# A Macaron block: down products summed up in three PSUM banks, one stretch of seven, other orders of blocks and loads

## The chip, the cores and the metric

The kernel runs on one core of a Trainium2 chip, in one launch. The metric is the device time in microseconds. It is given as the median of several runs; the profiled execution is one more run, with the hardware profiler on.

## The reference

All is in fp32. There are 8 sequences of 512 tokens with 512 features, and every sequence passes three layers one after another:

```python
x = x + 0.5 * ffn(layernorm(x), w_gate, w_up, w_down)
x = x + attention(layernorm(x), W_q, W_k, W_v, W_o)
x = x + 0.5 * ffn(layernorm(x), w_gate, w_up, w_down)      # same weights as above

def ffn(x, w_gate, w_up, w_down):                          # 512 -> 2048 -> 512
    h = silu(x @ w_gate) * (x @ w_up)
    g = h.reshape(..., 512, 4)
    h = keep the two of each four with the largest magnitude, 0 for the others
    return h @ w_down

def attention(x, ...):                                     # 16 heads of 32, 4 heads of K and V
    Q, K, V = x @ W_q, x @ W_k, x @ W_v                    # rotary embedding on Q and K
    return (softmax(Q @ K.T / sqrt(32)) @ V) @ W_o         # 16 query heads on 4 kv heads
```

## The kernel before, in words

**Blocks.** A feed-forward of one sequence is a block, so there are 16: `(b, 0)` is the first of sequence b, `(b, 1)` the second. The list `blocks` (L90) sets their order. Attention of a sequence and the layer norms of later blocks run beside the blocks as side stages: Python generators, one step at a time. The loop at L1047 takes the main groups of a block from `ffn` and advances a counter `n` by the group's size (1 stands for a full group of 8 fp32 matmuls with 256 columns, 0.5 for half of it). After each group, a side stage goes one step on when `n` has passed its due time. A block has `WIDTH = 42` units. `sides` (L1003) holds the first and last `n` of each stage: the layer norm of a block runs from 15 to 2 units before the block, and attention b in a window that L1007 to L1017 compute; a start more than 17 units into a block is moved to the next block's start.

**A planner writes every engine's order down.** `takes`, `waits`, `soon`, `later` and `fill` keep an estimate of when TensorE, VectorE (DVE) and ScalarE are free. DVE work that TensorE waits for goes into the queue `urgent`, other work into `put_off` and `for_later`. `fill` emits DVE work where the estimate says that it ends in time, and thinning steps last. `ensure` emits everything up to an entry at once. Each engine then runs in the order written down, and semaphores keep the data safe.

**Gate and up.** A block has four chunks c of 512 hidden features (`NCH = 4`), each with two woven pairs (`woven`, L613). A pair does two row groups as seven half-size products in place of eight (Strassen's scheme in Winograd's form). Their weights are quarters of w_gate and w_up or sums of quarters; the sums are made in the first block on DVE (`combine_gu`, L688, L693), stored in DRAM and later read from there. A pair holds a PSUM bank x through all of it, a bank v from its second to its fourth product, and a bank z near its end. There are three such banks for everything but attention's scores and outputs (`Bank`, L225, hands out the one that is free first).

**Thinning.** `keep_two_of_four` (L393) zeroes two of each four values of h, in two halves of 256 tokens: comparisons of magnitudes, then four `scalar_tensor_tensor` (L440) on DVE. It starts at the end of a chunk (`begin`, L757), which also emits every step that is left of the thinning before. At the end of a half, POOL (GpSimd) makes sums of quarters of h (L446 to L451).

**Down.** Two chunks together, an even and an odd one, make a pair g of chunks. Its product with w_down is again done as seven half-size products (`PRODUCTS`, L476, `products`, L532), each 8 matmuls into one bank, 3.45 us. 31 of the 32 pairs go this way; the last goes as plain products (`down`, L577). The right sides are quarters of w_down or sums of them (`SUMS`, L485), made once by POOL (`combine_down`, L492, L505) and kept in DRAM. `down_weights` (L510) loads them into three buffers: the load for product i+3 is issued after product i. Each product is added to one or two quarters of the tokens on DVE (L565), 12 additions for a pair. A quarter of h or of w_down is named by its row and column ("21" is the second row's first). The products of a pair are `owed`: `some(n)` yields the next n. Two of them stand inside the second woven pair of the following even chunk (after its fourth and fifth product), five after it.

**Attention** (L772). Side steps: loads (`wqkv`, `cs`), layer norm with transposes into `xT`, five projections and V, then for each of four groups of heads four steps of scores, maxima (`nm`, DVE), exponentials (ScalarE), weighted sums and a sum of exponentials (`total`, DVE), and at last four products with W_o. `xT` is one of two buffers that the blocks use too; the list `in_xT` lets no third one in. `p_slots` has two larger buffers (`cs`, `total`, `p`, and `raw` at the start); `wqkv` and `wo` share one.

All DMAs are issued by SP (SyncE), in the order written.

Of the kernel before, what the change touches and what calls it, by code (L numbers as in the profile page):

```python
# [26 lines left out]
def macaron_block(  # L27
# [62 lines left out]
    blocks = [(0, 0), (1, 0)]  # L90
    for b in range(2, B):
        blocks += [(b, 0), (b - 2, 1)]
    blocks += [(B - 2, 1), (B - 1, 1)]
# [184 lines left out]
    def layernorm_t(got, tag, src=None, xb=None):  # L278
# [34 lines left out]
        def turn(t):  # L313
            if t == 0:
                assert len(in_xT) < 2
                in_xT.append(got)
                got["xT"] = xtp.tile([P, ND, S], FP, tag="xT", name="xT")
            xT = got["xT"]
            tr = transposed([xn[t][:, c * P : (c + 1) * P] for c in range(ND)])
            nc.scalar.copy(xT[:, :, t * P : (t + 1) * P], tr.tile)  # L320
            tr.free(end=takes("act", 0.6, pe_heard()))
# [11 lines left out]
        if xb is None:  # L333
            there = at["pe"] + 10.0
            yield lambda: there
            found = [soon(0.9, partial(moments, t)) for t in (0, 1)]
            yield now
            found += [soon(0.9, partial(moments, t)) for t in (2, 3)]
            yield partial(when, found[:2])
            ensure(found[:2])  # L340
            scales((0, 1))
            yield partial(when, found)
            ensure(found)
            scales((2, 3))
            yield by_scalar
            for t in range(NT):
                normalise(t)
                end = at["act"]
                yield by_scalar if t < NT - 1 else lambda: max(end, by_scalar()) if len(in_xT) < 2 else None
# [43 lines left out]
    def keep_two_of_four(h, made, sums=None, halves=(0, 1)):  # L393
# [14 lines left out]
        for half in halves:  # L408
# [32 lines left out]
            if sums is not None:  # L441


                (h11, h21), (h12, h22) = ([h[:, i::2, :HALF], h[:, i::2, HALF:]] for i in range(2))
                if half == 0:
                    nc.gpsimd.tensor_tensor(sums[:, 2], h11, h12, ALU.add)  # L446
                else:
                    nc.gpsimd.tensor_tensor(sums[:, 1], h21, h22, ALU.add)
                    nc.gpsimd.tensor_tensor(sums[:, 0], h11, h22, ALU.add)
                    nc.gpsimd.tensor_tensor(h12, h12, h22, ALU.subtract)  # L450
                    nc.gpsimd.tensor_tensor(h21, h21, h11, ALU.subtract)  # L451
# [11 lines left out]
    def begin(steps):  # L463
# [20 lines left out]
    )  # L484
    SUMS = ("11+22", "12-22", "21-11", "11+12", "21+22")  # L485
# [6 lines left out]
    def combine_down(g):  # L492

        for c in range(2 * g, 2 * g + 2):
            raw = p_slots.tile([P, 4, D], FP, "raw")
            nc.sync.dma_start(out=raw, in_=w_down[c])
            there = at["pe"] + 12.0
            yield lambda: there
            yield now
            quarter = {f"{i + 1}{j + 1}": raw[:, i::2, j * HD2 : (j + 1) * HD2] for i in range(2) for j in range(2)}  # L500
            sums = wa_slots.tile([P, 6, 2, HD2], FP, "sums")

            for i, name in enumerate(SUMS):
                op = ALU.add if name[2] == "+" else ALU.subtract
                nc.gpsimd.tensor_tensor(sums[:, i], quarter[name[:2]], quarter[name[3:]], op)  # L505
                nc.sync.dma_start(out=combined[g, name][:, c % 2 * 2 : c % 2 * 2 + 2, :], in_=sums[:, i])
            yield now
        done_down.add(g)

    def down_weights(g, name):  # L510
        w = wdp.tile([P, 4, HD2], FP, tag="wd", name="wd")
        if (g, name) in combined:
            nc.sync.dma_start(out=w, in_=combined[g, name])
        else:
            i = int(name[0]) - 1
            for q in range(2):
                nc.sync.dma_start(
                    out=w[:, 2 * q : 2 * q + 2, :], in_=w_down[2 * g + q][:, i::2, i * HD2 : (i + 1) * HD2]
                )
        return w  # L520

    def ffn(b, final, last):
# [9 lines left out]
        def products(hs, g):  # L532

            operands = []
# [6 lines left out]
            def product(i):  # L541
                name, _, quarters = PRODUCTS[i]
                y = Bank([P, 2, HD2], "y")
                for t in range(2):
                    for n in range(4):
                        h, e = hs[n // 2]
                        if name in ("11+22", "21+22", "11+12"):
                            part = e[:, ("11+22", "21+22", "11+12").index(name), n % 2, :]
                        else:
                            row, col = int(name[0]) - 1, int(name[1]) - 1  # L550
                            part = h[:, 2 * (n % 2) + col, row * HALF : (row + 1) * HALF]
# [4 lines left out]
                            start=(n == 0),  # L556
                            stop=(n == 3),
                        )
# [4 lines left out]
                def add(half, side, sign, ends):  # L563
                    to = xb[:, 2 * half : 2 * half + 2, side * HD2 : (side + 1) * HD2]
                    nc.vector.scalar_tensor_tensor(to, y.tile, 0.5 * sign, to, ALU.mult, ALU.add)  # L565
                    if ends and g == NCH // 2 - 1 and i >= 5:
                        store(xb, (0, 1) if i == 5 else (2, 3))

                fill()
                y.free([soon(0.62, partial(add, *to, to == quarters[-1])) for to in quarters])  # L570
                written[b, final] = y.slot[1]
# [3 lines left out]
            return [(1 if i < 2 else 2, partial(product, i)) for i in range(len(PRODUCTS))]  # L575
# [112 lines left out]
        def combine_gu(i):  # L688
# [3 lines left out]
            def one(j, a, b, op):  # L692
                nc.vector.tensor_tensor(w[j], a, b, op)  # L693
                nc.sync.dma_start(out=gu_sums[i][:, j - S1], in_=w[j])

            gu_made[i] = [
                later(0.62, partial(one, j, w[a], w[b], op), at["pe"], for_later)
# [10 lines left out]
        for c in range(NCH):  # L708
# [27 lines left out]
            else:  # L736
                for pair in range(2):
# [7 lines left out]
                    for k, g in enumerate(groups):  # L745
                        yield g
                        if k == 2 and opens and i + 1 < 2 * NCH:
                            combine_gu(i + 1)

                        if pair == 1 and c % 2 == 0 and k in (3, 4):  # L750
                            yield from some(1)
# [4 lines left out]
                    if pair == 1:  # L756
                        begin(keep_two_of_four(h, list(last_one), e))  # L757
                        yield from some(5, False)
# [13 lines left out]
    def attention(b):  # L772
        ensure(written[b, 0])
        wa = wa_slots.tile([P, ND, D + 2 * KV], FP, "wqkv")
        for src, col in ((w_k, D), (w_q, 0), (w_v, D + KV)):
            nc.sync.dma_start(
                out=wa[:, :, col : col + src.shape[1]], in_=src.rearrange("(c p) n -> p c n", p=P)
            )
        cs = p_slots.tile([P, 4, S], FP, "cs")
        nc.sync.dma_start(out=cs[:, :2, :], in_=rope.rearrange("a p s -> p a s"))  # L780
        got = {}
        yield from layernorm_t(got, "xa", tokens[b][1])
# [5 lines left out]
        def projected(dst, col, scale):  # L788
# [16 lines left out]
            return [p_slots.used(w_slots.used(made))]  # L805
# [20 lines left out]
        in_xT.remove(got)  # L826
# [3 lines left out]
        nc.sync.dma_start(out=wo[:, :, :D], in_=w_o.rearrange("(c p) n -> p c n", p=P))  # L830
# [90 lines left out]
        for t in range(NT):  # L921
            found = scores(0, t, nm)
            yield partial(when, found)
# [79 lines left out]
    sides = [(11, 18, 6, partial(combine_down, 0), None, None), (22, 32, 6, partial(combine_down, 1), None, None)]  # L1003
# [3 lines left out]
    before = 0  # L1007
    for b in range(B):
# [6 lines left out]
        assert last - first > ATTENTION * 0.8  # L1015
        sides.append((first, last, ATTENTION, partial(attention, b), ("attention", b - 1) if b else None, ("attention", b)))
        before = last  # L1017
# [101 lines left out]
```

## Time and profile before

| what | us |
|---|---|
| median of three runs (3221.35 to 3228.51) | 3227.9 |
| the profiled execution: its time | 3222.35 |
| the profiled execution: span from first to last instruction | 3220.5 |
| TensorE (PE) matmul busy | 3180.1 |
| VectorE (DVE) busy | 2281.7 |
| ScalarE (ACT) busy | 1182.0 |
| GpSimd (POOL) busy | 608.1 |

The profile shows one execution. "Busy" is the time in which at least one instruction of an engine runs. In a row of a group the text before the bar names the line, the engine, the operation, what it writes and reads, its shape and the number of instructions; after it stand the busy time in all and the mean of one in ns; then the idle time of the engine just before these instructions, and what ended most of it. An fp32 matmul appears as two records. In a row of waits stand the waiting engine and tile, what it waited for, the total in us, how often, and the longest. A row of windows gives the stretch and its length, busy time (and instructions) of PE, weight load, DVE, ACT and POOL, the granted clock of TensorE, the DMA engines' busy share and GB/s. The granted clock is 0.999 over the span. A row of the timeline has the start, the length, the engine, the line and the instructions merged in it.

### The profile page before, as it was taken

How to read it: one execution, taken by the hardware profiler on the slowest of the kernel's cores; microseconds unless marked ns; L12 is line 12 of the kernel's file. 1: busy time of each engine (PE TensorE's matmuls, PEld its weight loads, DVE VectorE, ACT ScalarE, POOL GpSimd, SP SyncE). 2: the span in 40 equal slices, each digit the busy share in tenths (PEclk: the TensorE clock that was granted, in tenths of full speed). 3: DMA queues.
4: the chain of work that ended last, by engine and by line, in shares of the span. 5: the costliest groups of instructions: out<-in, count | busy, mean ns of one | idle time of the engine just before them, and what ended most of it. 6: DMA issues, size and time to landing. Idle time of an engine off the chain costs nothing.

```text
span 3220.5 us, 43674 instructions
## 1 busy us (share of the span) xinstructions
PE 3180.1 (99%) x15880; PEld 2320.9 (72%) x15880; DVE 2281.7 (71%) x4869; ACT 1182.0 (37%) x1669; POOL 608.1 (19%) x888
## 2 busy tenths in 40 slices
PE   8999999999999999999999999999999999999999
PEld 6886668766776677767776668666776668666886
DVE  6867875678577775887578766678577775787554
ACT  2222552145324441354314532145324542255211
POOL 2422011211221112111121112111120122201120
PEclk9999999999999999999999999999999999999999
DMA  7762345433533434434543345333533446234451
GB/s 241 245 215 95 113 145 171 138 116 111 194 111 122 157 121 160 138 125 150 166 140 122 119 155 197 120 108 113 202 102 121 156 124 214 95 112 147 152 172 46
DMA packets 249285, 463.21 MB, mean 144 GB/s; under 512 B 24432, under 2 KB 64368, under 8 KB 248304
## 3 DMA queue, kind: packets, MB, share of 16 engines
q1 hardware_dynamic: 249072, 460.42, 43.3%
q8 instruction: 127, 2.08, 0.3%
q14 instruction: 86, 0.70, 0.1%
HBM read 421.53 MB, written 38.80 MB: 143 GB/s over the span
## 4 chain that ended last, share of the span: by engine, by line
PE 94%; DVE 3%; DMA 1%; ACT 1%; issue 0%; SPq 0%; DVEq 0%; ACTq 0%
PE x L624 26%; PE y L552 23%; PE v L624 13%; PE z L624 6%; PE proj L792 4%; PE sc L838 4%; PE st L871 4%; PE ops L887 4%; PE y L972 3%; PE tr L262 2%; PE gu L599 1%; PE den L903 1%; PE vps L817 1%; PE y L582 1%; PE st L876 1%; DMA xn<-x 1%
## 5 line engine op out<-in xcount | busy, mean ns | idle before, releaser
L624 PE MATMUL x<-ts,w 128*128 128x256 f32 x3000 | 720.2, 383 | 6.2 <-DVE corner L638 5.9
L624 PEld LDWEIGHTS x<-ts,w 128*128 128x128 f32 x3000 | 561.0, 190 | 151.4 <-issue 48.1
L552 PE MATMUL y<-wd,h 128*128 128x256 f32 x1984 | 455.2, 383 | 9.0 <-DVE h L440 6.4
L552 PEld LDWEIGHTS y<-wd,h 128*128 128x128 f32 x1984 | 372.8, 190 | 97.2 <-issue 28.8
L446 POOL TENSOR_TENSOR e<-h 128x512 f32<-128x512 f32 x62 | 96.6, 1559 | 1495.7 <-DVE h L440 1364.5
L164 DVE TENSOR_REDUCE nm<-sc 128x1 f32<-128x512 f32 x512 | 320.8, 683 | 63.5 <-PE sc L838 62.0
L565 DVE SCALAR_TENSOR_TENSOR x<-y,x 128x512 f32<-128x512 f32 x372 | 242.2, 686 | 135.6 <-PE y L552 133.8
L552 PE MATMUL y<-wd,e 128*128 128x256 f32 x1488 | 335.3, 380 | 1.0 <-PE den L903 1.0
L552 PEld LDWEIGHTS y<-wd,e 128*128 128x128 f32 x1488 | 281.3, 190 | 53.5 <-issue 11.0
L164 DVE TENSOR_TENSOR total<-total,p 128x512 f32<-128x512 f32 x384 | 266.2, 734 | 58.2 <-ACT p L879 58.2
L879 ACT ACTIVATE p<-st 128x2048 f32<-128x2048 f32 x96 | 179.6, 1870 | 283.2 <-PE st L876 191.3
L254 ACT ACT_TABLE_LOAD x206 | 264.3, 1283 | 4.4 <-PEq L1108 0.7
L673 ACT ACTIVATE h<-x 128x256 f32<-128x256 f32 x125 | 47.5, 380 | 592.8 <-PE x L624 573.1
L242 ACT COPY row<-x 128x512 f32<-128x512 f32 x210 | 122.9, 585 | 383.2 <-PE x L624 382.3
L624 PE MATMUL v<-ts,w 128*128 128x256 f32 x1000 | 238.8, 382 | 3.5 <-ACT xT L320 2.9
L624 PE MATMUL x<-xT,w 128*128 128x256 f32 x1000 | 239.8, 383 | 0.0
L624 PE MATMUL z<-xT,w 128*128 128x256 f32 x1000 | 239.4, 382 | 0.0
L624 PE MATMUL v<-xT,w 128*128 128x256 f32 x1000 | 239.0, 382 | 0.4 <-ACT corner L242 0.4
L624 PEld LDWEIGHTS x<-xT,w 128*128 128x128 f32 x1000 | 186.4, 190 | 50.8 <-issue 24.0
L624 PEld LDWEIGHTS v<-ts,w 128*128 128x128 f32 x1000 | 187.6, 190 | 46.9 <-issue 15.1
L624 PEld LDWEIGHTS z<-xT,w 128*128 128x128 f32 x1000 | 186.4, 190 | 48.2 <-issue 20.9
L624 PEld LDWEIGHTS v<-xT,w 128*128 128x128 f32 x1000 | 187.3, 190 | 45.5 <-issue 11.8
(109 smaller groups left out, 4114.0 us busy)
## 6 DMA issues: line engine op xcount, KB each, us to landing
w<-gu SPq DMA_DIRECT2D x472, 256.0 KB, 3.3
w<-in_w_gu SPq DMA_DIRECT2D x394, 256.0 KB, 3.3
wd<-wd SPq DMA_DIRECT2D x155, 512.0 KB, 3.8
wd<-in_w_down SPq DMA_DIRECT2D x124, 256.0 KB, 4.9
x<-x SPq DMA_DIRECT2D x64, 256.0 KB, 2.6
xn<-x SPq DMA_DIRECT2D x64, 256.0 KB, 6.9
x<-in_x SPq DMA_DIRECT2D x32, 256.0 KB, 3.4
gu<-w SPq DMA_DIRECT2D x32, 256.0 KB, 2.6
```

The source lines that it names most:

```text
L164: self.does()
L242: nc.scalar.copy(dst, src)
L254: nc.scalar.activation(dummy[:, 1:2], dummy[:, 0:1], f)
L552: nc.tensor.matmul(out=y.tile[:, t, :], lhsT=part[:, t * P : (t + 1) * P], rhs=operands[i][:, n, :], start=(n == 0), stop=(n == 3),)
L565: nc.vector.scalar_tensor_tensor(to, y.tile, 0.5 * sign, to, ALU.mult, ALU.add)
L624: nc.tensor.matmul(out=bank.tile[:, m, :], lhsT=lhs[:, m, k, :], rhs=rhs[:, k, :], start=(first and m == 0 and k == 0), stop=(k == 1), ski ...
L792: nc.tensor.matmul(out=ps.tile, lhsT=wa[:, k, col : col + P], rhs=xT[:, k, :], start=(k == 0), stop=(k == ND - 1))
L838: nc.tensor.matmul(out=sc[:, kv, :], lhsT=qT[rows, c, t * P : (t + 1) * P], rhs=kT[rows, :], start=True, stop=True)
L871: nc.tensor.matmul(out=st[:, kv, :], lhsT=kT[rows, t * P : (t + 1) * P], rhs=qT[rows, c, :], start=True, stop=False)
L879: nc.scalar.activation(p, st, AF.Exp)
L887: nc.tensor.matmul(out=ops[rows, :], lhsT=v[:, t, rows], rhs=p[:, kv, :], start=(t == 0), stop=(t == NT - 1))
L972: nc.tensor.matmul(out=y.tile, lhsT=qT[:, k, t * P : (t + 1) * P], rhs=wo[:, k, :D], start=(k == 0), stop=(k == ND - 1))
```

## The change

The products of a pair of chunks follow another form of the scheme: seven products collect in three banks x, v and z, a bank is written on after it has been added to a quarter of the tokens, and each product is added once: 7 additions for 12. The sums of h are four for five, all after the second half, and the sums of w_down four for five; of w_down itself three quarters are used for two. All seven products stand in one stretch after the woven pair (`some(7)`).

Further: the order of the blocks; attention windows of equal width from one end to the other; attention's `xT` in `p_slots` in place of the blocks' buffers; attention's loads in smaller pieces, one per step; the raw chunks of w_down in four loads each; the sums of gate and up quarters due 3 us later in the planner.

```diff
-    blocks = [(0, 0), (1, 0)]
-    for b in range(2, B):
-        blocks += [(b, 0), (b - 2, 1)]
-    blocks += [(B - 2, 1), (B - 1, 1)]
+    first_of = {0: 0, 1: 1, 2: 2, 3: 3, 5: 4, 8: 5, 9: 6, 11: 7}
+    second_of = {4: 0, 6: 1, 7: 2, 10: 3, 12: 4, 13: 5, 14: 6, 15: 7}
+    blocks = [(first_of[i], 0) if i in first_of else (second_of[i], 1) for i in range(2 * B)]
...
             if t == 0:
-                assert len(in_xT) < 2
-                in_xT.append(got)
-                got["xT"] = xtp.tile([P, ND, S], FP, tag="xT", name="xT")
+                if tag == "xf":
+                    assert len(in_xT) < 2
+                    in_xT.append(got)
+                    got["xT"] = xtp.tile([P, ND, S], FP, tag="xT", name="xT")
+                else:
+                    got["xT"] = p_slots.tile([P, ND, S], FP, "xT")
...
-                (h11, h21), (h12, h22) = ([h[:, i::2, :HALF], h[:, i::2, HALF:]] for i in range(2))
-                if half == 0:
-                    nc.gpsimd.tensor_tensor(sums[:, 2], h11, h12, ALU.add)
-                else:
-                    nc.gpsimd.tensor_tensor(sums[:, 1], h21, h22, ALU.add)
-                    nc.gpsimd.tensor_tensor(sums[:, 0], h11, h22, ALU.add)
-                    nc.gpsimd.tensor_tensor(h12, h12, h22, ALU.subtract)
-                    nc.gpsimd.tensor_tensor(h21, h21, h11, ALU.subtract)
+                (h11, h21), (_, h22) = ([h[:, i::2, :HALF], h[:, i::2, HALF:]] for i in range(2))
+                if half == 1:
+                    nc.gpsimd.tensor_tensor(sums[:, 0], h21, h22, ALU.add)
+                    nc.gpsimd.tensor_tensor(sums[:, 1], sums[:, 0], h11, ALU.subtract)
+                    nc.gpsimd.tensor_tensor(sums[:, 2], h[:, 1::2, :HALF], sums[:, 1], ALU.subtract)
+                    nc.gpsimd.tensor_tensor(h21, h11, h21, ALU.subtract)
...
     PRODUCTS = (
-        ("11", "12-22", ((0, 1, 1), (1, 1, 1))),
-        ("11+12", "22", ((0, 0, -1), (0, 1, 1))),
-        ("22", "21-11", ((0, 0, 1), (1, 0, 1))),
-        ("21+22", "11", ((1, 0, 1), (1, 1, -1))),
-        ("11+22", "11+22", ((0, 0, 1), (1, 1, 1))),
-        ("12-22", "21+22", ((0, 0, 1),)),
-        ("21-11", "11+12", ((1, 1, 1),)),
+        ("11", "11", "x", (0, 0)),
+        (0, "12-11", "v", (1, 1)),
+        (1, "22-T1", "x", (0, 1)),
+        (2, "22", "v", (0, 1)),
+        ("21", "22-12", "x", (1, 1)),
+        ("12", "21", "z", (0, 0)),
+        ("22", "21-T2", "x", (1, 0)),
     )
-    SUMS = ("11+22", "12-22", "21-11", "11+12", "21+22")
+    SUMS = ("12-11", "22-T1", "22-12", "21-T2")
...
-            nc.sync.dma_start(out=raw, in_=w_down[c])
-            there = at["pe"] + 12.0
-            yield lambda: there
-            yield now
+            for r in range(4):
+                nc.sync.dma_start(out=raw[:, r], in_=w_down[c][:, r])
+                there = at["pe"] + 5.0
+                yield now if r < 3 else lambda: there
...
-                y = Bank([P, 2, HD2], "y")
+                first, last = name not in used, name not in [p[2] for p in PRODUCTS[i + 1 :]]
+                if first:
+                    used[name] = Bank([P, 2, HD2], name)
+                else:
+                    waits(ensure(taken[name]))
+                y = used[name]
...
-                            start=(n == 0),
+                            start=(first and t == 0 and n == 0),
...
-                y.free([soon(0.62, partial(add, *to, to == quarters[-1])) for to in quarters])
-                written[b, final] = y.slot[1]
+                taken[name] = [soon(0.62, add)]
+                if last:
+                    y.free(taken[name])
+                written[b, final] = taken[name]
...
-            return [(1 if i < 2 else 2, partial(product, i)) for i in range(len(PRODUCTS))]
+            return [(2, partial(product, i)) for i in range(len(PRODUCTS))]
...
+            there = at["pe"] + 3.0
             gu_made[i] = [
-                later(0.62, partial(one, j, w[a], w[b], op), at["pe"], for_later)
+                later(0.62, partial(one, j, w[a], w[b], op), there, for_later)
...
-                        if pair == 1 and c % 2 == 0 and k in (3, 4):
-                            yield from some(1)
...
-                        yield from some(5, False)
+                        yield from some(7, False)
...
-        for src, col in ((w_k, D), (w_q, 0), (w_v, D + KV)):
-            nc.sync.dma_start(
-                out=wa[:, :, col : col + src.shape[1]], in_=src.rearrange("(c p) n -> p c n", p=P)
-            )
-        nc.sync.dma_start(out=cs[:, :2, :], in_=rope.rearrange("a p s -> p a s"))
+        for src, col in ((w_k, D), (w_v, D + KV)):
+            loads.append((wa[:, :, col : col + KV], src.rearrange("(c p) n -> p c n", p=P)))
+        for i in range(2):
+            loads.append((cs[:, i], rope[i]))
+        for k in range(ND):
+            loads.append((wa[:, k, :D], w_q[k * P : (k + 1) * P, :]))
...
-        yield from layernorm_t(got, "xa", tokens[b][1])
+        for ready in layernorm_t(got, "xa", tokens[b][1]):
+            if loads:
+                dst, src = loads.popleft()
+                nc.sync.dma_start(out=dst, in_=src)
+            yield ready
...
-        nc.sync.dma_start(out=wo[:, :, :D], in_=w_o.rearrange("(c p) n -> p c n", p=P))
...
             found = scores(0, t, nm)
+            nc.sync.dma_start(out=wo[:, t, :D], in_=w_o[t * P : (t + 1) * P, :])
...
-    sides = [(11, 18, 6, partial(combine_down, 0), None, None), (22, 32, 6, partial(combine_down, 1), None, None)]
+    sides = [(10, 19, 10, partial(combine_down, 0), None, None), (22, 34, 10, partial(combine_down, 1), None, None)]
...
-        left = place(B - 1, 1) - 13 - before
-        first = max(before, place(b, 0) + WIDTH + 16)
-        if first % WIDTH > 17:
-            first += WIDTH - first % WIDTH
-        last = min(place(b, 1) - 13, max(before + left / (B - b), first + 1.4 * WIDTH))
+    bounds = [WIDTH + 16 + b * (place(B - 1, 1) - 13 - WIDTH - 16) / B for b in range(B + 1)]
```

More of the change, by code (lines that the diff above doesn't have):

```diff
@@ L89, in macaron_block @@
     gu_sums = [dram.tile([P, 4, 2, ND // 2, P], FP, name=f"gu_{i}") for i in range(2 * NCH)]
-    blocks = [(0, 0), (1, 0)]
-    for b in range(2, B):
-        blocks += [(b, 0), (b - 2, 1)]
-    blocks += [(B - 2, 1), (B - 1, 1)]
+    first_of = {0: 0, 1: 1, 2: 2, 3: 3, 5: 4, 8: 5, 9: 6, 11: 7}
+    second_of = {4: 0, 6: 1, 7: 2, 10: 3, 12: 4, 13: 5, 14: 6, 15: 7}
+    assert B == 8
+    blocks = [(first_of[i], 0) if i in first_of else (second_of[i], 1) for i in range(2 * B)]
     coming = deque()
@@ L348, in layernorm_t @@
                 end = at["act"]
-                yield by_scalar if t < NT - 1 else lambda: max(end, by_scalar()) if len(in_xT) < 2 else None
+                yield by_scalar if t < NT - 1 else (
+                    lambda: max(end, by_scalar()) if tag == "xa" or len(in_xT) < 2 else None
+                )
             for t in range(NT):
@@ L503, in combine_down @@
             for i, name in enumerate(SUMS):
-                op = ALU.add if name[2] == "+" else ALU.subtract
-                nc.gpsimd.tensor_tensor(sums[:, i], quarter[name[:2]], quarter[name[3:]], op)
+                of = quarter[name[3:]] if name[3:] in quarter else sums[:, int(name[4:]) - 1]
+                nc.gpsimd.tensor_tensor(sums[:, i], quarter[name[:2]], of, ALU.subtract)
                 nc.sync.dma_start(out=combined[g, name][:, c % 2 * 2 : c % 2 * 2 + 2, :], in_=sums[:, i])
@@ L514, in down_weights @@
         else:
-            i = int(name[0]) - 1
+            i, j = (int(digit) - 1 for digit in name)
             for q in range(2):
                 nc.sync.dma_start(
-                    out=w[:, 2 * q : 2 * q + 2, :], in_=w_down[2 * g + q][:, i::2, i * HD2 : (i + 1) * HD2]
+                    out=w[:, 2 * q : 2 * q + 2, :], in_=w_down[2 * g + q][:, i::2, j * HD2 : (j + 1) * HD2]
                 )
@@ L532, in products @@
         def products(hs, g):
-            operands = []
+            operands, used, taken = [], {}, {}
             assert g in done_down
@@ L541, in product @@
             def product(i):
-                name, _, quarters = PRODUCTS[i]
-                y = Bank([P, 2, HD2], "y")
+                side, _, name, (half, col) = PRODUCTS[i]
+                first, last = name not in used, name not in [p[2] for p in PRODUCTS[i + 1 :]]
[4 more added lines that the diff above has]
+                y = used[name]
                 for t in range(2):
@@ L546, in product @@
                         h, e = hs[n // 2]
-                        if name in ("11+22", "21+22", "11+12"):
-                            part = e[:, ("11+22", "21+22", "11+12").index(name), n % 2, :]
-                        else:
-                            row, col = int(name[0]) - 1, int(name[1]) - 1
-                            part = h[:, 2 * (n % 2) + col, row * HALF : (row + 1) * HALF]
+                        if isinstance(side, int):
+                            part = e[:, side, n % 2, :]
+                        else:
+                            row, place = int(side[0]) - 1, int(side[1]) - 1
+                            part = h[:, 2 * (n % 2) + place, row * HALF : (row + 1) * HALF]
                         nc.tensor.matmul(
@@ L555, in product @@
                             rhs=operands[i][:, n, :],
-                            start=(n == 0),
+                            start=(first and t == 0 and n == 0),
                             stop=(n == 3),
+                            skip_group_check=True,
                         )
@@ L561, in product, with add @@
                 xb = xs[b, final]
[L563 to L566, printed above, removed]
+                def add():
+                    to = xb[:, 2 * half : 2 * half + 2, col * HD2 : (col + 1) * HD2]
+                    nc.vector.scalar_tensor_tensor(to, y.tile, 0.5, to, ALU.mult, ALU.add)
+                    if g == NCH // 2 - 1 and i in (5, 6):
                         store(xb, (0, 1) if i == 5 else (2, 3))
                 fill()
-                y.free([soon(0.62, partial(add, *to, to == quarters[-1])) for to in quarters])
-                written[b, final] = y.slot[1]
+                taken[name] = [soon(0.62, add)]
+                if last:
+                    y.free(taken[name])
+                written[b, final] = taken[name]
             for _ in range(3):
                 load()
-            return [(1 if i < 2 else 2, partial(product, i)) for i in range(len(PRODUCTS))]
+            return [(2, partial(product, i)) for i in range(len(PRODUCTS))]
         def down(h, w, c, t):
@@ L774, in attention @@
         wa = wa_slots.tile([P, ND, D + 2 * KV], FP, "wqkv")
-        for src, col in ((w_k, D), (w_q, 0), (w_v, D + KV)):
-            nc.sync.dma_start(
-                out=wa[:, :, col : col + src.shape[1]], in_=src.rearrange("(c p) n -> p c n", p=P)
-            )
         cs = p_slots.tile([P, 4, S], FP, "cs")
-        nc.sync.dma_start(out=cs[:, :2, :], in_=rope.rearrange("a p s -> p a s"))
-        got = {}
-        yield from layernorm_t(got, "xa", tokens[b][1])
+        loads = deque()
+        for src, col in ((w_k, D), (w_v, D + KV)):
[4 more added lines that the diff above has]
+            loads.append((wa[:, k, :D], w_q[k * P : (k + 1) * P, :]))
+        got = {}
+        for ready in layernorm_t(got, "xa", tokens[b][1]):
[3 more added lines that the diff above has]
+            yield ready
         xT = got["xT"]
@@ L804, in projected @@
             made = soon(0.65, partial(nc.vector.tensor_tensor, dst, dst, sw, ALU.add))
-            return [p_slots.used(w_slots.used(made))]
+            return [p_slots.used(w_slots.used(made), 1)]
         of_k = projected(kT, D, 1.0)
@@ L825, in attention @@
         fill()
-        in_xT.remove(got)
         nc.scalar.copy(v, vps.tile)
@@ L1006, in macaron_block @@
         sides.append((place(b, i) - 15, place(b, i) - 2, NORM, stage, ("attention", b) if i else None, None))
-    before = 0
-    for b in range(B):
-        left = place(B - 1, 1) - 13 - before
-        first = max(before, place(b, 0) + WIDTH + 16)
-        if first % WIDTH > 17:
-            first += WIDTH - first % WIDTH
-        last = min(place(b, 1) - 13, max(before + left / (B - b), first + 1.4 * WIDTH))
-        assert last - first > ATTENTION * 0.8
+    bounds = [WIDTH + 16 + b * (place(B - 1, 1) - 13 - WIDTH - 16) / B for b in range(B + 1)]
+    for b, (first, last) in enumerate(zip(bounds, bounds[1:])):
+        assert place(b, 0) + WIDTH + 16 <= first and last <= place(b, 1) - 13
         sides.append((first, last, ATTENTION, partial(attention, b), ("attention", b - 1) if b else None, ("attention", b)))
-        before = last
     sides.sort(key=lambda s: s[0])
```

## The prediction

> **What bounds the kernel now.** I read the page's busy shares and its chain first, then the groups, then what TensorE waited for, then windows of the stretches in which it waited, and last the timeline there.
>
> ```profile
> PE 3180.1 (99%) x15880; PEld 2320.9 (72%) x15880; DVE 2281.7 (71%) x4869; ACT 1182.0 (37%) x1669; POOL 608.1 (19%) x888
> ...
> PE 94%; DVE 3%; DMA 1%; ACT 1%; issue 0%; SPq 0%; DVEq 0%; ACTq 0%
> ...
> L552 PE MATMUL y<-wd,h 128*128 128x256 f32 x1984 | 455.2, 383 | 9.0 <-DVE h L440 6.4
> ...
> L446 POOL TENSOR_TENSOR e<-h 128x512 f32<-128x512 f32 x62 | 96.6, 1559 | 1495.7 <-DVE h L440 1364.5
> ...
> L565 DVE SCALAR_TENSOR_TENSOR x<-y,x 128x512 f32<-128x512 f32 x372 | 242.2, 686 | 135.6 <-PE y L552 133.8
> ```
>
> TensorE is busy 99% of the span and the chain runs over it for 94%. So only two things can save time: fewer matmuls, or fewer of the few waits between them. L565 is the row that shrinks most, but it is on DVE, 71% busy, and it waited for TensorE 133.8 us rather than the other way round.
>
> ```profile
> PE y L552 <- DVE h L440: 6.4, 5, 2.5
> PE x L624 <- DVE corner L638: 5.9, 4, 4.7
> PE tr L262 <- DVE z L854: 3.6, 2, 1.8
> PE sc L838 <- DVE nm L164: 3.4, 3, 1.4
> PE v L624 <- ACT xT L320: 2.9, 2, 1.5
> ...
> PE y L552 <- DMA wd<-wd: 0.6, 1, 0.6
> ```
>
> ```profile
> 560.00:800.00 240.00, 232.63 (x1227) 160.51 (x1229) 181.66 (x384) 93.97 (x128) 40.05 (x68) 1.00 0.39 126
> 2000.00:2240.00 240.00, 231.95 (x1203) 160.94 (x1202) 178.87 (x378) 93.51 (x127) 39.83 (x68) 0.99 0.39 129
> 1200.00:1440.00 240.00, 240.00 (x1199) 174.70 (x1197) 173.76 (x370) 79.52 (x115) 47.09 (x72) 1.00 0.43 142
> ```
>
> No DMA wait is of any size. TensorE idles 7.4 and 8.0 us in the first two windows, and in the third, equally long, not at all. I also followed the matmuls from start to start: records within a product are 0.216 us apart (two for each fp32 matmul, so a down product of 8 takes 3.45 us). Taking every step wider than usual for its kind, without the 0.1 us after each switch between 32-row and full-array matmuls, gives 39.0 us of waiting: 13.8 in the first 160 us, 8.2 in 560 to 800, 9.2 in 2000 to 2240, 7.8 in all the rest. This is the whole stake, 1.2%.
>
> **The change part by part.**
>
> *Matmuls.* A part pair keeps 7 products of 8 matmuls (31 pairs x 7 x 8 x 2 records = the 3472 rows of L552). Switches stay too: 33 tiled steps in each attention, 264 in all. Cost 0.
>
> *Seven additions for twelve.* 31 x 5 x 0.686 = 106 us less DVE work. It lies beside TensorE and counts only where DVE is late, below.
>
> *Four sums of h for five.* L446, 97 us of POOL, goes; all four now follow half 1. POOL is 19% busy. What counts is the deadline: products "11" and "11+12" used to need half 0 alone and to stand inside the woven pair; now the second product needs half 1 and one POOL sum (1.3 us, L448). The timeline shows the present form of this wait:
>
> ```profile
> 702.13 1.43 DVE L440 SCALAR_TENSOR_TENSOR h<-m,h 128x256 f32<-128x256 bf16 x4
> ...
> 702.95 2.23 PE L552 MATMUL y<-wd,h 128*128 128x256 f32 x8 [2.45 <-DVE h L440]
> ```
>
> I took, for each of the 31 pairs, the thinning work of the odd part still undone where the stretch would begin (two products earlier than the present third product, 3.45 us each, and the attention steps between). It is 0 to 1.3 us in 22 pairs, 2.8 in two, and above that in seven: 7.4 (first), 4.8, 6.2, 4.4, 6.2, 4.8, 4.8. The first product hides 3.45, and the second reads the odd part only half-way in (0.86), less the sum and its signal (1.5): 2.8 us are covered, and 1.4 us of DVE work (two additions) is gone by then. The excess over 4.2 us is 3.2 + 0.6 + 2.0 + 0.2 + 2.0 + 0.6 + 0.6; the two of 2.0 lie in the windows 560 to 800 and 2000 to 2240, which the new pace thins out (0.6 each). Together 6.4 us, as much as the 6.4 us that goes. Net 0; between -6 (additions saved win) and +29 (no credit, 16 pairs at 2.2).
>
> *Three banks, one product in between.* Each product waits for the addition of the last but one; before, three banks rotated. The row first: product by product, the first addition starts 0.04 us after the product's end in the median, 1.55 at four in five, over 2.4 in 8 of 217. With 0.69 us each it ends within 2.2 us, and 3.45 are there. [...] Were one bank reused at once, each of 124 reuses (four per pair) would cost 0.7 to 2.2 us, 90 to 270 us; with a product in another bank between them, by the row, nearly nothing. I go by the row: the 8 late ones at up to 1.4 us, some no longer late: +2 us, ends 0 and +12. Behind them side steps find one bank free, not three, as they do in the woven products now.
>
> *Weights of the down products.* Two parts of w_down itself become three, sums five to four. A part comes as two DMAs of 1 KB rows: landing 4.9 us (wd<-in_w_down), against 3.8 for a sum (wd<-wd); SP takes 0.56 us for an issue. The fourth product's load is issued after the first product, so 6.9 us before its use; by the row it lands after 5.5. [...] If a fifth landed as the slowest tenth does (6.2, so 6.8 in all), the two loads of a pair would still just fit; and in the stretch no gate/up load is under way. I take the row: +0.5, ends 0 and +12 (62 loads late by 0.2).
>
> *Gate/up sums due 3 us later, raw weights in quarters.* In the first block DVE, in order, waited for a quarter behind a 1 MB load of w_down, and TensorE behind DVE:
>
> ```profile
> 60.35 4.92 DVE L693 TENSOR_TENSOR w<-w 128x512 f32<-128x512 f32 x3 [4.01 <-DMA w<-in_w_gu]
> ...
> 67.12 3.47 PE L624 MATMUL x<-ts,w 128*128 128x256 f32 x8 [4.70 <-DVE corner L638]
> ```
>
> The sum at 60.35 ran out only as the load landed; put 3 us later, its place is behind the addition that TensorE wanted. Four POOL sums of 20 go. I count 4.5 of 4.9 us. SP issues 16 raw loads for 4 and 16 stores for 20. Ends 0 and -7 (1.7 us at 102.7 may go too).
>
> *Blocks' order, attention paced evenly.* In units of a full product group (3.45 us) the attentions now take 55, 59, 72, 72, 65, 58.8, 69.1 and 69.1; afterwards all 69.9. The waits of 560 to 800 and 2000 to 2240 are those of the second and sixth attention: 59 units each, beginning at a block's start. Without the thinning (2.6 each) they are 12.0 us. The six others lose 7.8 us in all, so 1.2 each is left: -9.6. The first, at 55, waits little, so density is not all of it; phase matters, and the new third and sixth begin 29 units into a block, where none did. Ends -12 and +8.
>
> *Attention's loads and xT.* Loads go from 5 to 12 (56 more in all, 0.33 us each on SP), spread over steps; wo's no longer stands waiting for vps with gate/up loads behind it. No product waits for these now: 0, ends -1 and +3. xT in p's slots waits for nothing that is not long done; the attention's start is freed from the two xT buffers. The last projection reads xT before p is written; that order is in TensorE's own stream. 0.
>
> **Sum**: 0 + 2 + 0.5 - 4.5 - 9.6 = -11.6 us. The profiled execution took 3222.35 us (span 3220.5, 1.9 around it) and would take 3210.7. It was a quick one: the three runs have the median 3227.9. The same difference from the median gives 3216.
>
> **Rivals.** *Waits only move* (0.29): the early deadline eats what the even pace gives, +6 to +12 instead of 0. For it: the seven late pairs, DVE without a gap in them. Against: 24 pairs have room. Time 3225. *The deadline becomes the bound* (0.23): even pacing puts each attention's dense part over two pairs, 16 in all. DVE has then, for 7 units of woven products with attention, 12.8 us of thinning, 7.5 of woven work and some 12.7 of attention, 33 of 34 us (7 x 3.45 and some 10 of attention's matmuls). If 5 us are left at the stretch's start, the second product waits 2.2 us in each: +35 for 6.4, against -14.1 and +2.5 elsewhere: +17, 3245. It decides from 3.9 us left on average (18 us of waiting in all). Against it: pairs at 69 to 72 units leave 2.8 to 4.8 today, with four more additions in DVE's way. *Nothing is done by the additions*, and only start and pace count: within the first case. *Larger gain* is part of it too: at most the 35 us that are not the first transposes' wait.
>
> **How the numbers follow.** 0.3% (9.7 us) is about what a measurement of this kernel can tell from no change. The likeliest case spreads from -27 to -10: 0.48 faster. Waits that move: 0.29 within 0.3%. Deadline: 0.23 slower. The likeliest case's own range is 3201 to 3218; to leave out no more than 2 in 10 it must reach the better part of the rival: 3202 to 3240.
>
> **What would show it.** The products (now L552) still have 3472 records, the additions (now L565) 217, POOL no sum in half 0. TensorE's wait for corner at L638 is under 1.5 us; windows of 240 us all have TensorE over 237 busy; waits of the down products for h or for a POOL sum stay under 8 us in all, for their own additions under 4. It is wrong if the second product of a stretch waits for e in more than eight pairs by over 1 us, or products wait for x additions or weights in most stretches.

## The result, and the profile after

| | before | after |
|---|---|---|
| median of six runs each, us | 3226.63 | 3213.43 |
| lowest and highest | 3221.35 to 3228.51 | 3210.11 to 3214.43 |
| the profiled execution, its time | 3222.35 | 3210.11 |
| its span | 3220.5 | 3208.2 |

The ratio is 0.9963, with a 95% interval of 0.9953 to 0.9973: faster by 0.37%, some 12 us. The prediction had 3216 for the median and 3210.7 for the profiled execution.

The page of the kernel after, in the order in which the page of before was read: busy shares, the chain by engine, the down products (now into banks x and v; L561), POOL's sums of h (L452).

```profile
PE 3176.9 (99%) x15880; PEld 2322.4 (72%) x15880; DVE 2189.8 (68%) x4718; ACT 1195.8 (37%) x1683; POOL 507.2 (16%) x822
...
PE 96%; DVE 2%; DMA 1%; ACT 1%; POOL 0%; issue 0%; SPq 0%; POOLq 0%; DVEq 0%
...
L561 PE MATMUL x<-wd,h 128*128 128x256 f32 x1488 | 339.9, 382 | 0.0
...
L561 PE MATMUL v<-wd,e 128*128 128x256 f32 x992 | 228.2, 382 | 7.1 <-POOL e L452 4.0
...
L452 POOL TENSOR_TENSOR e<-h 128x512 f32<-128x512 f32 x62 | 79.3, 1279 | 2232.5 <-DVE h L446 1892.9
```

The count of matmuls is as before, x15880, and DVE has 92 us less to do. Of the three products that read a sum of h, the two into v (v<-wd,e) have idle time before them, 7.1 us in 992 records; the one into x has none. The additions are now three groups with their banks in the name, 124 + 62 + 31 = 217 (the groups with shapes kept apart):

```profile
L575 DVE SCALAR_TENSOR_TENSOR x<-x 128x512 f32<-128x512 f32 x124 | 85.4, 689 | 78.3 <-PE x L561 77.4
...
L575 DVE SCALAR_TENSOR_TENSOR x<-v,x 128x512 f32<-128x512 f32 x62 | 42.6, 686 | 25.5 <-PE v L561 25.1
...
L575 DVE SCALAR_TENSOR_TENSOR x<-z,x 128x512 f32<-128x512 f32 x31 | 21.4, 691 | 32.1 <-PE z L561 32.0
```

What TensorE waited for:

```profile
PE tr L263 <- DVE xn L373: 7.4, 3, 6.4
PE v L561 <- POOL e L452: 4.0, 4, 1.5
PE st L886 <- DVE nm L165: 3.1, 2, 1.5
PE v L561 <- DMA wd<-in_w_down: 2.9, 1, 2.9
...
PE x L636 <- DVE corner L650: 1.4, 2, 1.2
```

The rows of before for sc<-nm (3.4) and tr<-z (3.6) are gone. The down products' wait for h (6.4, five times) became one for POOL's sum (4.0, four times). No row has a product waiting for an addition. Of the down products' rows one is new: the weights, once, 2.9 us. Elsewhere the wait of st for maxima grew from 0.6 to 3.1 us. The two stretches in which before lost most (columns as in the windows shown ahead):

```profile
560.00:800.00 240.00, 238.46 (x1231) 171.83 (x1230) 170.51 (x357) 90.51 (x125) 34.26 (x64) 1.00 0.42 132
2000.00:2240.00 240.00, 238.46 (x1295) 167.38 (x1294) 181.21 (x389) 104.21 (x137) 33.36 (x44) 1.00 0.41 130
```

TensorE idles 1.5 us in each, where it idled 7.4 and 8.0. Counted from matmul start to start as in the prediction, the waits are 27.5 us (12.7 in the first 160 us, 14.8 behind them), against 39.0 (13.9 and 25.1). This count, "waits in all", is used below for every kernel. It is 11.5 us less, of 12.3 us of span, but where a kernel has stretches at half clock it takes in some of the matmuls slowed there. The rows of TensorE's waits alone add up to 36.2 us before and 27.5 after, 8.7 us less. Before also has two stretches of 3.41 us at half clock (last section), which cost 3.4 us, and the profiled execution of after has none. Together that is 12.1 of the 12.3 us.

### The profile page after: what moved, and what is told of

The parts are those of the page before. It is cut to its first block, busy times and chain, and to the rows that moved or that the text cites. A ratio compares the mean times of both kernels' runs of the same rounds, so it can differ in the third digit from the quotient of the medians.

```text
span 3208.2 us, 43276 instructions
## 1 busy us (share of the span) xinstructions
PE 3176.9 (99%) x15880; PEld 2322.4 (72%) x15880; DVE 2189.8 (68%) x4718; ACT 1195.8 (37%) x1683; POOL 507.2 (16%) x822
## 4 chain that ended last, share of the span: by engine, by line
PE 96%; DVE 2%; DMA 1%; ACT 1%; POOL 0%; issue 0%; SPq 0%; POOLq 0%; DVEq 0%
PE x L636 27%; PE v L636 13%; PE x L561 13%; PE z L636 7%; PE v L561 6%; PE proj L809 4%; PE st L886 4%; PE sc L853 4%; PE ops L902 4%; PE y L988 3%; PE z L561 3%; PE tr L263 1%; PE gu L611 1%; PE den L918 1%; PE vps L834 1%; PE st L891 1%
## 5 line engine op out<-in xcount | busy, mean ns | idle before, releaser
L452 POOL TENSOR_TENSOR e<-h 128x512 f32<-128x512 f32 x62 | 79.3, 1279 | 2232.5 <-DVE h L446 1892.9
L561 PE MATMUL x<-wd,h 128*128 128x256 f32 x1488 | 339.9, 382 | 0.0
L165 DVE TENSOR_TENSOR total<-total,p 128x512 f32<-128x512 f32 x384 | 273.8, 749 | 81.1 <-ACT p L894 81.1
L561 PEld LDWEIGHTS x<-wd,h 128*128 128x128 f32 x1488 | 280.2, 190 | 62.5 <-issue 19.3
L561 PE MATMUL v<-wd,e 128*128 128x256 f32 x992 | 228.2, 382 | 7.1 <-POOL e L452 4.0
L561 PEld LDWEIGHTS v<-wd,e 128*128 128x128 f32 x992 | 186.2, 190 | 52.6 <-issue 13.3
L407 ACT ACTIVATE a<-h 128x1024 f32<-128x1024 f32 x128 | 134.9, 1054 | 186.0 <-DVE m L425 106.8
```

The source lines that it names most:

```text
L165: self.does()
L407: nc.scalar.activation(a, h[:, :, half * HALF : (half + 1) * HALF], AF.Abs)
L561: nc.tensor.matmul(out=y.tile[:, t, :], lhsT=part[:, t * P : (t + 1) * P], rhs=operands[i][:, n, :], start=(first and t == 0 and n == 0), ...
```

## The experiments

The theory was the prediction's: the pace gives most, the start some, the down products nothing. Its rivals: the additions saved on DVE give the time; the windows do little; parts cancel each other. Each kernel was timed in rounds with the kernel before on the same chip (its medians were 3224.9, 3224.8 and 3224.7 in the three groups).

**One part at a time on the kernel before.**

*e1_pace*: the blocks' order, the even windows, `xT` in `p_slots`.

```diff
+    bounds = [WIDTH + 16 + b * (place(B - 1, 1) - 13 - WIDTH - 16) / B for b in range(B + 1)]
...
+                    got["xT"] = p_slots.tile([P, ND, S], FP, "xT")
```

> The kernel before, with the new order of blocks, even attention windows and attention's xT in p's slots alone. Theory 'pace' (the gain is that of the even pace): TensorE's waits after the first 160 us fall from 25 us to 13 to 17, the time by 8 to 12 us (ratio 0.9965 to 0.9975). Theory 'DVE relief' (the gain is that of 106 us less work on DVE and of the stretch): DVE stays as loaded as before, so the waits stay above 22 us and the time within 3 us of before.

Measured: 3232.2, ratio 1.0023 (1.0014 to 1.0032), so 7 us slower. Waits in all are 45.2. Its waits:

```profile
PE y L558 <- DMA wd<-wd: 10.0, 4, 4.6
...
PE st L876 <- DVE nm L165: 6.7, 4, 1.9
PE x L630 <- DVE corner L644: 6.7, 2, 6.5
```

The rows sc<-nm and tr<-z are gone, so the pace does thin the dense stretches out; the time goes to a new row, the down products' weights. Its timeline at one of the two places (start, length, engine and line, xcount, idle before):

```profile
903.13 0.42 SPq L782 DMA_DIRECT2D wqkv<-in_w_k  x1
903.61 0.50 SPq L782 DMA_DIRECT2D wqkv<-in_w_q  x1
904.15 0.51 SPq L782 DMA_DIRECT2D wqkv<-in_w_v  x1
904.77 0.56 SPq L786 DMA_DIRECT2D cs<-in_rope  x1
905.38 3.28 SPq L287 DMA_DIRECT2D xn<-x  x4
908.76 2.87 SPq L519 DMA_DIRECT2D wd<-wd  x2
...
917.56 2.00 PE L558 MATMUL y<-wd,h 128*128 128x256 f32 x5 [4.47 <-DMA wd<-wd]
```

An attention starts 29 units into a block. At that moment all its loads but w_o's are issued, one of them the 1 MB of w_q; the weights of a product stand behind them in SP's order and arrive late. The other place is at 1965 us. The windows of before began 0 to 17 units into a block. Only the fourth (1217 us) issued its loads among down products, between the first and the second, where woven work still stands between the products: the next weights, issued at 1222.8 us behind the loads, had 9 us until their product, which did not wait. In e1 those issued at 908.8 had 4 us.

*e2_down*: the down scheme alone, seven products in one stretch.

> The kernel before, with the down products in three banks, seven additions, four sums and one stretch alone. Theory 'pace': the two dense stretches keep their waits (some 8 us each), the early deadline costs them 1 to 3 us more: time from 2 us less to 5 us more than before. Theory 'DVE relief': DVE comes through the dense stretches earlier, 8 to 12 us less than before.

Measured: 3226.4, ratio 1.0006 (0.9997 to 1.0015), no difference that can be told. Waits in all are 39.3. The wait of the products for h (6.4) became one for POOL's sums (4.1), the rows sc<-nm and tr<-z stayed as they were, and the wait for corner grew from 5.9 to 13.0 us, 7.0 of it in the first 160 us. Behind them it is 6.0 us in four waits, where before has 0.9; what causes these stays open:

```profile
PE x L630 <- DVE corner L644: 13.0, 7, 2.8
...
PE v L555 <- POOL e L446: 4.1, 5, 1.1
PE tr L262 <- DVE z L858: 3.6, 2, 1.8
PE sc L842 <- DVE nm L164: 3.4, 3, 1.4
```

*e3_start*: the sums of gate and up due 3 us later, the raw weights in four loads.

> The kernel before, with the raw weights in quarters and gate/up sums due 3 us later alone. By the prediction's step: 4.5 us less, all in the first 160 us. By the trace after the change, where the first 160 us lose 12.7 us for 13.9: 0 to 2 us less, since waits of 1.4 and 1.6 us stand in the place of the one of 4.9. If the later 3.1 us wait for down weights belongs to the stretch and not to these edits, it is missing here and the gain is 3 to 4.5.

Measured: 3227.9, ratio 1.0008 (1.0000 to 1.0017). Waits in all are 43.7. Its row x<-corner fell to 2.8 from 5.9, as argued, but three waits came in the same stretch: v<-corner 3.0, x<-row 1.8, tr<-row 1.1. Alone, none of these three parts gains: +7, +1.5 and +3 us, the last two within or at the edge of the noise. The small loads were not tried alone.

**One part taken out of the kernel after.**

*e4_old_windows*: after, with the loop of before for the attention windows (they come to 59, 62, 59, 70, 70, 59, 69, 69 units).

> The kernel after, with the attention windows computed as before (with the new order they are 59, 62, 59, 70, 70, 59, 69 and 69 units wide; three of 59 begin at or near a block's start). Theory 'pace': waits come back, 3 to 8 us for each window of 59 to 62 units that begins at a block's start: 6 to 16 us more than after, equal to before or nearly. Theory 'DVE relief': no more than 3 us more than after.

Measured: 3223.8, ratio 0.9999 (0.9990 to 1.0008): some 12 us of the gain gone.

```profile
PE v L561 <- POOL e L452: 10.3, 9, 2.0
...
PE sc L853 <- DVE nm L165: 4.1, 4, 1.4
PE tr L263 <- DVE z L869: 3.6, 2, 1.8
```

The dense rows are back at about the sizes of before (3.4 and 3.6), and the wait for POOL's sum, which itself waits for the end of the thinning on DVE, is 10.3 us in nine stretches in place of 4.0 in four.

*f1_pace_loads* and *f2_no_loads* test the new cause. f1 is e1 with the attention's loads in small pieces; f2 is after with these loads as before.

```diff
+        for ready in layernorm_t(got, "xa", tokens[b][1]):
+            if loads:
+                dst, src = loads.popleft()
+                nc.sync.dma_start(out=dst, in_=src)
+            yield ready
```

> The kernel before, with the order of blocks, even windows and xT in p's slots (as e1_pace) and attention's loads in small pieces, one per step; down products, start as before. Theory 'pace needs the small loads': e1_pace waited 10.0 us for weights of the down products (wd), twice 4.6 us right behind a megabyte of w_q and lost the clock each time; these go, the waits after the first 160 us fall from 30 to 17 to 21 us, and the time to 4 to 9 us below before (ratio 0.997 to 0.9988). Rival 'pace needs the down change': the waits stay near 28 us and the time at or above before's.

> The kernel after, with attention's loads as before (w_q, w_o, rope in one piece each, all issued at the stage's start). Theory 'pace needs the small loads': waits for wd of 4 to 5 us come back in the third and the sixth attention, which begin 29 units into a block, with a dip of the clock behind each: 10 to 16 us more than after. Rival 'pace needs the down change': less than 3 us more than after.

Measured: f1 3218.6, ratio 0.9981 (0.9972 to 0.9990); f2 3229.5, ratio 1.0015 (1.0006 to 1.0023). So the small loads are worth 13.6 us on e1, and 17 us in the kernel after (0.9962 against 1.0015 of 3225). In f1 the row y<-wd is 0.6 for 10.0 and waits in all are 35.9. In f2 the waits for weights are back at both attentions (6.2 and 4.3; the 3.8 is the wait of the first 160 us that after has too, there 2.9):

```profile
PE x L561 <- DMA wd<-wd: 6.2, 1, 6.2
...
PE z L561 <- DMA wd<-in_w_down: 4.3, 1, 4.3
PE v L561 <- DMA wd<-in_w_down: 3.8, 1, 3.8
```

In the profiles f2 takes 19.5 us more than after. These waits are 11.4 us of it (14.3 less the 2.9), and three stretches at half clock, of which after has none, 8.5 us (granted clock 0.997 over the span, 1.000 in after); 3.4 of these follow the wait of the first 160 us, before any attention. The new loads are smaller, spread over steps and in another order, all at once; which of these does it was not separated.

*f3_twelve*: after, with five more additions for each pair (of zero times the product), planned as such.

```diff
+                    if i < 5:
+                        nc.vector.scalar_tensor_tensor(to, y.tile, 0.0, to, ALU.mult, ALU.add)
...
-                taken[name] = [soon(0.62, add)]
+                taken[name] = [soon(1.24 if i < 5 else 0.62, add)]
```

> The kernel after, with twelve DVE additions per pair in place of seven: the first five products are added once more, with the factor 0, so that only the work is added (106 us of DVE in all, known to the planner). Theory 'DVE work is covered': 0 to 4 us more than after, most of it as waits of a product for a bank. Theory 'DVE relief': 8 to 13 us more.

Measured: 3221.9, ratio 0.9991 (0.9982 to 1.0000), 9 us slower than after. Waits in all are 36.8; of the 9.3 us more, 8.4 lie behind the first 160 us. Two stretches at half clock cost 3.4 us besides (granted clock 0.999). The longest of the rows that grew or are new:

```profile
PE st L888 <- DVE nm L165: 7.1, 6, 1.9
...
PE x L638 <- ACT row L243: 2.8, 1, 2.8
...
PE v L561 <- DVE m L437: 2.1, 1, 2.1
...
PE x L561 <- DVE x L577: 1.1, 2, 0.7
```

Only 1.1 us of it is a bank held longer by the second addition. The rest is what is late elsewhere: maxima of scores (7.1 for 3.1; f1, with its twelve additions, has 6.7), woven work, thinning. So in the kernel after, five additions less per pair are worth time although DVE is busy 68% of the span.

**The start, the banks, and a better version.**

*f4_late_quarters*: after, with the loads of gate and up quarters of the first block after the fourth product of the stretch. The 2.9 us for weights in the profile after are the following (its timeline; two loads of w_down's part issued behind four quarters):

```profile
97.89 1.26 POOL L452 TENSOR_TENSOR e<-h 128x512 f32<-128x512 f32 x1 [2.78 <-DVE h L446]
99.17 2.87 SPq L115 DMA_DIRECT2D w<-in_w_gu  x4
...
102.50 1.20 SPq L521 DMA_DIRECT2D wd<-in_w_down  x2
...
108.47 1.90 PE L561 MATMUL v<-wd,e 128*128 128x256 f32 x7 [2.95 <-DMA wd<-in_w_down]
```

> The kernel after, where the first block's loads of eight gate/up quarters, issued just before the stretch of down products, come after the fourth of the seven products. If the 3.1 us wait for down weights at 105 us stands behind those 2 MB, it goes and nothing else changes: 2 to 4 us less than after. If it is the writing and reading again of the sums of w_down, it stays: within 1 us of after.

Measured: 3209.1, ratio 0.9953 (0.9941 to 0.9966). No row has a product waiting for in_w_down any more; waits of the first 160 us are 11.6 for 12.7, in all 27.2. One product waits 0.9 us for an addition in this profile. In time f4 can't be told from after.

*g3_no_start*: after without the start edits (raw weights in one load, sums not put later). *g4_after*: after, unchanged, in the same group of runs.

> The kernel after, with the raw weights in one piece and gate/up sums due at once, as before. By the prediction's step 4.5 us more than after. By the traces (first 160 us: 13.3 us of waiting in e2_down, 12.7 in after): 0 to 2 us more, or less than after.

> The kernel after itself, unchanged, on the same chip as the three others: a ratio to before of 0.995 to 0.9973, against which they are read.

Measured: g3 3213.5, ratio 0.9966 (0.9953 to 0.9978); g4 3210.9, ratio 0.9962 (0.9950 to 0.9975). g4's waits in all are 27.7, and unlike the profile after it has one stretch at half clock (1.7 us; granted clock 0.999). In waits the start edits give 2.0 us in the first 160 us (14.9 to 12.9); g3's x<-corner is 6.0 for 2.1. In time the two can't be told apart.

*g2_bank_at_once*: after with the fifth and sixth product changed over, so that bank x is written again with no product in another bank between, once in each pair.

```diff
-        ("21", "22-12", "x", (1, 1)),
         ("12", "21", "z", (0, 0)),
+        ("21", "22-12", "x", (1, 1)),
```

> The kernel after, with the sixth product (in z) and the fifth (in x) changed over, so that the fifth and the seventh follow one another in the bank x with no product between: 31 times the seventh waits for the addition of the fifth. By the additions' delays before the change (0.04 us in the median from the product's end to the start, 0.69 for the addition, some 0.3 for the signals): 1 us each at least, 31 to 70 us more than after in all. If the wait were hidden (side steps in between, TensorE's queue): under 10 us more.

Measured: 3230.5, ratio 1.0021 (1.0012 to 1.0030), 19.6 us slower than g4. Its waits begin with a row that after does not have:

```profile
PE x L561 <- DVE x L575: 12.5, 14, 3.6
```

A bare reuse cost 0.95 us (some ten of the 14), 0.26 more than the addition's 0.69, and one 3.6; the other 17 pairs have no such row. Waits in all are 44.8, 17.1 above g4.

*g1_order*: f4 with the rows of `PRODUCTS` in the order 0, 5, 2, 1, 4, 3, 6, the product into z second, so that POOL has one product more of time before its first sum is read.

> The kernel after with late quarters (f4_late_quarters), and the seven products in the order 0, 5, 2, 1, 4, 3, 6: x in each second place as now, but the product that needs half 0 of h alone (12 by 21) stands second, and POOL's sums are needed one product later. If the early deadline still costs what the trace shows (POOL's sum e waited for 4 times, 4.1 us), these waits go: 3 to 6 us less than after. If DVE is the limit there and not POOL's sum, the wait only moves to the next product: within 1 us of f4_late_quarters.

Measured: 3208.7 (3207.4 to 3210.6), ratio 0.9953 (0.9940 to 0.9965). The wait for POOL's sum is 1.5 us once, for 4.0 in four; waits in all are 25.7, the least of all kernels. It is the best version, 2 us below g4, with intervals that overlap.

Not tried: the new products at the old places inside the woven pair. There the woven x and z and the products' x and v would need four of three banks.

## Why the prediction was right, and where its sum was not

The total was right: -11.6 predicted, -12.3 of span measured, 0.37% for 0.36%. That was partly luck. Two terms set to 0 were large, the pace term could not stand without one of them, four more were off by 2 to 3 us, and no term stood for the clock, though the sum was one of waits alone: the waits fell by some 9 us, and 3.4 us are half clock that before has and the profiled execution of after has not.

- **Matmuls 0**: right, x15880 in both. The span without the rows of waits and the half-clock time is 3180.9 us before and 3180.7 after.
- **Attention's loads 0, ends -1 and +3**: the step that failed. "No product waits for these now" was true of before, where attentions began 0 to 17 units into a block and only the fourth had weights behind its loads, due 9 us later. The pace moves two starts to 29 units into a block, next to down products. The prediction named that phase as the reason for the +8 at the end of the pace term, but did not carry it to the queue: the loads issued there stand ahead of the weights. e1, f1 and f2 show it: 10.0 us of waits, and 13.6 to 17 us of time, half clock included.
- **Pace -9.6**: it holds with the small loads only. Pace, `xT` and loads together (f1) take 4.4 us off the waits behind the first 160 us, and 6 us off the time (ratio 0.9981); the windows in after are worth 12 us (e4). The pace without the loads is +7 (e1), near the term's upper end. One of the widths named is wrong: by L1007 to L1017 the eighth attention of before has 55 units like the first (562 to 617), not 69.1; the -9.6 does not use it.
- **Additions 0**: mis-sized. f3 gives 9 us, in the kernel after. The argument was that DVE at 71% waits for TensorE, which is an average. In the dense attention stretches DVE is the late one (in before TensorE waits there twice 2.45 us for h, 3.6 for z and 3.4 for maxima), and there each addition that goes is time that maxima and thinning get back (f3, with the work added again: st<-nm 7.1 for 3.1). On before alone (e2) this did not show: its windows keep the attention dense, and the waits of 3.4 and 3.6 us there remain. That the old windows hide the gain is argued, not shown, as e2 has its new waits for corner too.
- **Deadline 0 (6.4 for 6.4)**: measured 4.0 for 6.4, in four stretches for the seven that I listed. The sum and its signal, put at 1.5 us, took 1.33 (1.28 in the mean, and 0.05 from its end to the matmul that waited). The rival "the deadline becomes the bound" decided from 18 us of waits and was far off; with the windows of before it came nearer, 10.3 in nine (e4).
- **Three banks +2**: 0.0 measured; the groups of after show additions that wait for products and no product that waits for one. The row (0.04 us from product to addition) was the right one to go by. Counted again in the trace of before, it leaves more room than was read from it: 0.04 us at four in five too, 1.6 only at nineteen in twenty, over 2.4 in 3 of 217. g2 shows the other side: a bank used again at once cost 19.6 us with 31 reuses, 0.95 us for a bare one, inside the 0.7 to 2.2 named. With one product of 3.45 us between, as in the kernel after, no product waits for an addition.
- **Weights +0.5**: 2.9, in one place, behind gate and up quarters in the first block (not the short rows of w_down: these loads of 256 KB landed at 3.6 us in the median after, the sums, 512 KB each, at 5.4).
- **Start -4.5**: about -2.0 of waits (g3 against g4), and from before to after only -1.2, as the wait of 2.9 for weights and one of 1.6 for POOL's sum at 97 us lie in that stretch too. The wait of 4.7 for corner did go. Alone on before it was +3 (e3).

Going by ratios, on 3225 us and step by step from before to after: pace +7, its loads -13.5, down scheme -5 (f1 to g3), start -1 to -3. The down scheme was forecast at +2.5. Its -5 is less than the 9 us of f3, and the intervals of f1 and g3 just overlap, so its size is known only roughly.

## What to carry to other kernels

When work that issues loads is moved, list which loads then stand ahead of which deadline in the same issue order; a burst of bulk loads that made no product wait at one phase cost 17 us at another, and issuing it in pieces, one per step, removed that. The busy share of an engine that is not the bound says nothing about the stretches in which it is late: test a saving there by adding the same work back (f3), not by its average. Edits that gain nothing alone can gain together; so take parts out of the whole as well as trying them singly, before one is dropped.

## What the runs showed of the hardware that was not expected

Some waits of TensorE are followed by a stretch at half clock. Windows of before and of e1, with the granted clock in the third column from the end:

```profile
66.00:71.00 5.00, 3.88 (x11) 3.23 (x12) 5.00 (x16) 0.38 (x2) 0.00 (x0) 0.66 0.99 363
...
700.00:705.00 5.00, 2.55 (x11) 1.64 (x10) 4.64 (x17) 4.63 (x8) 1.36 (x2) 1.00 0.21 56
2148.00:2153.00 5.00, 5.00 (x16) 4.01 (x16) 2.92 (x8) 1.18 (x4) 4.86 (x4) 0.66 0.00 0
```

```profile
918.00:923.00 5.00, 5.00 (x18) 4.08 (x17) 0.03 (x1) 0.00 (x0) 0.00 (x0) 0.66 0.00 1
1969.00:1977.00 8.00, 6.84 (x18) 5.57 (x19) 0.14 (x1) 0.00 (x0) 0.00 (x0) 0.57 0.03 11
```

0.66 over 5 us is 3.4 us at 0.5, and 0.57 over 8 us is 6.9 us at 0.5. In before the clock is 0.50 from 66.72 to 70.13 us and from 2148.85 to 2152.26, and the records of a product start 0.427 us apart there, against 0.216 at full clock. So each stretch costs up to half its length, 1.7 or 3.4 us, on top of the wait. Before has two (after the wait of 4.9 us at 62, and after one of 2.6 at 2144.8), e1 four, f2 three, after none in its profiled execution. Taking half of their length and the rows of TensorE's waits off the span leaves 3179 to 3184 us in all fourteen profiles, so the kernels differ in little else.

It is not the wait's length alone. 2.6 us at 700 in before left the clock at 1.00, and so did 2.9 us in after, up to 108.47 (1.00 from 105 to 115); the 2.6 us at 2144.8 and 2.0 us in e1 at 1796.6 were followed by half clock (in e1 0.98 over 1760 to 1800 and 0.97 over 1800 to 1840). What else decides is not shown. Removing a wait can so save more than the wait: from before to the profiled execution of after it is 3.4 us beside the 8.7 of the waits.
